# Selected rows taken batch by batch: the first batch's attention among the first attention's units, its feed-forward beside the last ranks, the second batch's attention with keys and values

## The chip, the cores and the metric

The kernel runs on one core of one Trainium2 chip. The metric is the device time of one execution in microseconds (us). Three runs of the kernel before took 1828.56, 1829.37 and 1838.12 us (median 1829.37). A fourth execution was profiled; all views below are of that one.

## What is computed

Two layers of a gated model on x of shape (2, 2048, 512), each with a cross-attention onto a context of 128 tokens and a feed-forward; every part is added to x through tanh of a gate. Cut to what matters here:

```python
x = x + tanh(g_xattn[0]) * L0_xattn(layernorm(x), ctx)   # 16 heads of 32
x = x + tanh(g_ffn[0]) * L0_ffn(layernorm(x))
x = x + tanh(g_xattn[1]) * L1_xattn(layernorm(x), ctx)   # 16 heads of 64
x = x + tanh(g_ffn[1]) * L1_ffn(layernorm(x))            # ternary weights, convolution

def L0_ffn(x):
    _, idx = top_k(x @ w_router, 256)             # of each batch's 2048 rows
    x_sel = x[idx]
    h = rmsnorm(x_sel, g1)
    x_attn = causal_attention(h) @ W_out.T        # 16 heads of 32, 256 rows
    h2 = rmsnorm(x_sel + x_attn, g2)
    x_ff = (silu(h2 @ W1.T) * (h2 @ W2.T)) @ W3.T # 1365 hidden columns
    return x with rows idx set to x_sel + x_attn + x_ff
```

So only 256 rows of each batch go through the attention and feed-forward of `L0_ffn`. The other rows get a cheap affine step. Which rows are selected is known for a batch only when all of its 2048 scores are.

## The kernel before, in words

All x rows are held as tiles of 128 rows by 512 columns, 32 of them; four make a block of 512 rows, and there are eight blocks, four for each batch. All matrix products are float32, but for the ternary feed-forward of the second layer and the counting of ranks (bfloat16). PE below is TensorE, with PEld its weight loads; DVE is VectorE, ACT ScalarE, POOL GpSimd, SP SyncE, whose queue issues nearly all DMAs, in order.

**First attention** (`cross_attention`, called at L647). It runs over 128 units, a unit being one head of one block (L338). A unit does scores (L271), softmax (a maximum on DVE L116, four exponentials on ACT L119, a reciprocal on DVE L127, a multiplication on POOL L128), transposes of the probabilities (L289) and, for four heads together, values (L297). The front of the next block, that is its norm and its transposed rows (L110), is issued at unit 8 of a block (`ahead`), the queries (L248) group by group, and the output products (L315) of a finished block are spread over the units after it. Products for queries, output and row transposes go through a pool of two PSUM buffers (`ps_mm`), transposes and values through another of two (`ps_o`), scores through one of four (`ps_sc`).

**Router and ranks.** When a block's output is done, `after_block` (L649) puts a generator `router` (L447) into `pending`. `beside` (L441) advances it by two steps in each unit. It takes the norm's statistics and the router's score of each row, writes the rows to `x1_d` and the rows after the affine step to `x_d`, and then counts each row's rank by comparisons on DVE (L511) and matmuls with ones (L517). After the last block of a batch, `gather` (L591) turns ranks into row indices (L597, L601, L617) and fetches the 256 rows into `xs` by an indirect DMA on POOL's queue (L619). The second batch's last router, ranks and gather run in a loop of their own after the units (L651).

**Selected rows** (L659 to L985), both batches side by side, 512 columns wide. Weights are loaded (L718, L722, `load_ffn` L665), masks built on POOL, then: norm of the rows, transposes (L110), values (L751), and for each of four chunks of four heads queries and keys (L769), scores with mask for either batch (L788, L798, L799), exponentials (L804), a multiplication on POOL (L814), transposes (L824), values (L829). Then output (L852), the second norm (L694, L698, L703), and the feed-forward in eleven steps of 128 hidden columns: up and gate (L952), SiLU and product (L960, L962), down (L938). Beside the feed-forward the second layer's two weight matrices are made ternary (`ternary`, L879): load, sum of absolute values on ACT, a sum across partitions on PE (L901), and integers on ACT and DVE. The results are added into `x_d` by indirect DMAs (L979).

**Keys and values of the second attention** (`W1.keys_values()` at L989; L182, L200), and then that attention with the ternary feed-forward's first half as a second stream of work (`beside4`), and at the end the second half.

**What sets the order.** The program is written in terms of tiles; a scheduler puts each engine's instructions into one fixed order and adds the waits. The order of the Python code gives the priority: what is issued earlier stands earlier where it can. A tile pool with so many buffers makes the next user of a buffer wait for the last reader of it, and a pool that is opened where another was closed waits for the instructions that used that place.

Of the kernel before, what the change touches and what calls it, by code (L numbers as in the profile page):

```python
# [10 lines left out]
F32 = mybir.dt.float32  # L11
BF16 = mybir.dt.bfloat16
# [31 lines left out]
def flamingo_kernel(ctx: ExitStack, tc: tile.TileContext, a: dict, out: bass.AP):  # L44
# [28 lines left out]
    dramp = ctx.enter_context(tc.tile_pool(name="dramp", bufs=1, space=bass.MemoryType.DRAM))  # L73

# [61 lines left out]
    class CrossWeights:  # L136
# [38 lines left out]
        def keys_values(self):  # L175
            L, nE, bias = self.L, self.nE, self.bias
            with ExitStack() as st:
                ps0 = psum_pool(st, L + "ps0", 2)
                for e in range(nE):
                    pk = ps0.tile([P, B * M], F32, name="pk", tag="pk")  # L180
                    for c in range(CC):
                        nc.tensor.matmul(  # L182
                            pk,
                            self.wk[:, c, ts(e, P)],
                            self.ctxT[:, c, :],
                            start=(c == 0),
                            stop=(c == CC - 1),
                        )
                    src = pk.rearrange("p (b m) -> p b m", b=B)
                    if bias:  # L190
                        nc.vector.tensor_scalar(
                            self.kT[:, :, e, :], src, self.bk[:, e : e + 1], None, ALU.add
                        )
                    else:
                        nc.vector.tensor_copy(self.kT[:, :, e, :], src)
                for b in range(B):
                    for n in range(nE * P // 512):
                        pv = ps0.tile([P, 512], F32, name="pv", tag="pv")
                        for c in range(CC):
                            nc.tensor.matmul(  # L200
                                pv,
                                self.ctxT[:, c, ts(b, M)],
                                self.wv[:, c, ts(n, 512)],
                                start=(c == 0),
                                stop=(c == CC - 1),
                            )
                        to = self.v[:, b, ts(n, 512)]
                        if bias:
                            nc.vector.tensor_tensor(to, pv, self.bv[:, ts(n, 512)], ALU.add)
                        else:  # L210
                            nc.scalar.copy(to, pv)
# [179 lines left out]

    with ExitStack() as st:
        xres = st.enter_context(tc.tile_pool(name="xres", bufs=1))
        x = [xres.tile([P, D], F32, name=f"x{i}") for i in range(NT)]
        rp = st.enter_context(tc.tile_pool(name="router", bufs=1))
# [39 lines left out]
        def load_x(i):  # L435
            for t in range(i * TB, (i + 1) * TB):
                nc.sync.dma_start(out=x[t], in_=x_in[t])

        pending = []

        def beside(u):  # L441

            for _ in range(2):
                while pending and next(pending[0], pending) is pending:
                    pending.pop(0)

        def router(n, tiles):  # L447
# [6 lines left out]
            for i in range(TB):  # L454
# [4 lines left out]
                ws = act.tile([P, D], F32, name="ws2", tag="ws2", bufs=1)  # L459
# [21 lines left out]
            for i in range(TB):  # L481
                yield
                xo = act.tile([P, D], F32, name="xo", tag="xo", bufs=2)
# [7 lines left out]
                nc.sync.dma_start(out=x_d[b][ts(t0 + i - b * TPB, P), :], in_=xo)  # L491
            yield
# [98 lines left out]
        def gather(b):  # L591
# [26 lines left out]
            for r in range(2):  # L618
# [7 lines left out]
                )  # L626

        W0 = CrossWeights("L0_", D // P, True, gx[0], st, "left")
        with ExitStack() as st0:
            W0.load_context(st0, "left")  # L630
            load_x(0)
            W0.load_rest()
            for i in range(1, B * NBLK):
                load_x(i)
            W0.keys_values()
        act = st.enter_context(tc.tile_pool(name="L0_act", bufs=2))
        row = st.enter_context(tc.tile_pool(name="L0_row", bufs=8))
        ps_mm = psum_pool(st, "L0_mm", 2)
        ps_sc = psum_pool(st, "L0_sc", 4)
        ps_o = psum_pool(st, "L0_o", 2)  # L640

        def stage1_rows(n):
            tiles = x[n * TB : (n + 1) * TB]
# [4 lines left out]
            W0, act, act, ps_mm, ps_sc, ps_o, row, 2, 8, stage1_rows,  # L648
            lambda n, tiles: pending.append(router(n, tiles)), beside,  # L649
        )  # L650
        while pending:  # L651
            beside(None)


    right, right1, right2 = ExitStack(), ExitStack(), ExitStack()
    step = const.tile([P, 2], F32, name="step")
    finstep = const.tile([P, 1], F32, name="finstep")
    w2_d = dramp.tile([P, HC, D], BF16, name="w2_d")
    with ExitStack() as st:  # L659
        AHEAD = 3  # L660
        wst = st.enter_context(tc.tile_pool(name="wst", bufs=AHEAD))
        keepp = st.enter_context(tc.tile_pool(name="keepp", bufs=1))
        w13 = {}

        def load_ffn(f):  # L665
            n = min(P, DFF - f * P)
            w1c = wst.tile([P, DC, P], F32, name="w1c", tag="w1c")
            nc.sync.dma_start(
                out=w1c[:, :, :n], in_=row_tiles(a["W1T"])[:, :, ds(f * P, n)]
            )  # L670
            w2c = wst.tile([P, DC, P], F32, name="w2c", tag="w2c")
            nc.sync.dma_start(
                out=w2c[:, :, :n], in_=row_tiles(a["W2T"])[:, :, ds(f * P, n)]
            )
            w3c = wst.tile([P, D], F32, name="w3c", tag="w3c")
            nc.sync.dma_start(out=w3c[:n, :], in_=a["W3T"][ds(f * P, n), :])
            w13[f] = (w1c, w2c, w3c)

        g1 = keepp.tile([P, DC], F32, name="g1")
        nc.sync.dma_start(out=g1, in_=a["g1"])  # L680
        g2 = keepp.tile([P, DC], F32, name="g2")
        nc.sync.dma_start(out=g2, in_=a["g2"])
        xa = [keepp.tile([P, D], F32, name=f"xa{i}") for i in range(4)]

        def wide(name):
            return keepp.tile([P, DC, BLK], F32, name=name, tag="wide", bufs=2)

        def rms_block(tiles, gcol, dst, pool, ps, tag, name, r=None):

            hn = [pool.tile([P, D], F32, name="hn", tag="hn", bufs=4) for _ in tiles]  # L690
            if r is None:
                ss = pool.tile([P, 4], F32, name=name + "_ss", tag="rms_ss")
                for i, t in enumerate(tiles):
                    nc.scalar.activation(hn[i], t, AF.Square, accum_out=ss[:, i : i + 1])  # L694
                rs = rsqrt(4, ss, 1.0 / D, 1e-6, small, name + "_r")
                r = [rs[:, i : i + 1] for i in range(4)]
            for i, t in enumerate(tiles):
                nc.vector.tensor_scalar(hn[i], t, r[i], None, ALU.mult)  # L698
            transpose_block(
                ps,  # L700
                tag,
                hn,
                lambda d, pt: nc.vector.tensor_scalar(  # L703
# [732 lines left out]
```

## Time and profile before

| | us |
|---|---|
| median of 3 runs | 1829.37 |
| the profiled execution | 1832.29 |
| its span, first to last instruction | 1830.2 |
| PE busy | 1663.7 |
| DVE busy | 1278.9 |
| ACT busy | 1046.0 |
| POOL busy | 524.2 |
| last output product of the first attention ends | 512.3 |
| first row transposes of the second attention | 813.4 |

The page of the profile gives busy times by engine, then the span in 40 slices (45.8 us each here) as digits of tenths. The busy time of PE is modelled and holds the latency of matmuls, so a busy PE need not be at its peak; the granted clock beside it says how fast its clock was let run (1.00 is full). A line of the instructions in order of time has the start, the length of the merged run, engine, line, operation, output tile<-inputs, shape, number of records, and in brackets the idle time of the engine before it and what ended it. Every float32 matmul shows as two records, each with its weight load.

### The profile page before, as it was taken

The page shows a single profiled execution, that of the slowest core. Times are in us where ns is not written, and L with a number is a line of the kernel's source. Part 1 is how long each engine was busy: PE and PEld are TensorE (multiplying, and loading weights), DVE is VectorE, ACT ScalarE, POOL GpSimd, SP SyncE. Part 2 cuts the span into 40 slices and gives each one's busy share as a digit, 9 for nine tenths or more (in the row PEclk, how much of TensorE's full clock was granted, in tenths as well). Part 3 has the DMA queues.
Part 4 walks back from the last instruction along what each step waited for, and adds up shares of the span by engine and source line. Part 5 has one row for each costly group of instructions (what it writes and reads, how often), then busy time and mean ns, then how long its engine had stood idle before and what let it go on. Part 6 is the DMA issues. An engine that isn't in the chain of part 4 may idle for free.

```text
span 1830.2 us, 24658 instructions
## 1 busy us (share of the span) xinstructions
PE 1663.7 (91%) x7836; PEld 832.5 (45%) x7882; DVE 1278.9 (70%) x2591; ACT 1046.0 (57%) x3057; POOL 524.2 (29%) x668
## 2 busy tenths in 40 slices
PE   6989998899958989989999999999998999898969
PEld 3544444444424444445544444544444454443423
DVE  5777777977674622234447789799888888876966
ACT  1654545355402526115447778778777887854566
POOL 4543344253211210042224243322424243221200
PEclk9989989999968889989999999999999999999989
DMA  8010001010152037240011234234143133155475
GB/s 291 7 41 35 30 35 41 24 47 36 53 191 102 1 123 236 81 115 24 7 41 64 87 115 147 93 135 141 48 155 113 81 101 130 69 206 214 144 237 189
DMA packets 98455, 184.36 MB, mean 101 GB/s; under 512 B 11327, under 2 KB 30527, under 8 KB 94614
## 3 DMA queue, kind: packets, MB, share of 16 engines
q1 hardware_dynamic: 97430, 180.70, 28.5%
q0 software_dynamic: 896, 2.10, 0.6%
q8 instruction: 62, 1.02, 0.2%
q14 instruction: 67, 0.55, 0.1%
HBM read 108.31 MB, written 74.45 MB: 100 GB/s over the span
## 4 chain that ended last, share of the span: by engine, by line
PE 36%; DVE 12%; DMA 6%; ACT 5%; issue 2%; POOL 2%; SPq 1%; POOLq 0%; DVEq 0%; ACTq 0%
PE pp L315 8%; PE pq L248 8%; PE ph L1079 3%; DVE h L1095 3%; PE po L297 2%; PE sc L271 2%; PE pu L952 2%; PE acc L938 2%; PE pw L952 2%; PE tp L289 2%; PE po L1308 2%; DMA x<-h_d 1%; DMA h_d<-h 1%; DMA hf<-h_d 1%; DMA hq<-hq_d 1%
## 5 line engine op out<-in xcount | busy, mean ns | idle before, releaser
L119 ACT ACTIVATE A<-sc,nmx 128x128 f32<-128x128 f32 x1024 | 363.6, 382 | 147.8 <-DVE nmx L116 122.5
L128 POOL TENSOR_TENSOR A<-A,rden 128x512 f32<-128x512 f32 x256 | 274.6, 1075 | 471.5 <-DVE rden L127 361.6
L315 PE MATMUL pp<-L_wo,OT 128*128 128x512 f32 x768 | 362.4, 604 | 4.9 <-DVE u L1089 4.5
L248 PE MATMUL pq<-xnT,L_wq 128*128 128x512 f32 x768 | 346.7, 600 | 0.2 <-ACT xnT L237 0.2
L119 ACT ACTIVATION_READ_ACCUMULATOR A<-sc,nmx 128x1 f32 x1024 | 225.9, 221 | 0.0
L116 DVE TENSOR_REDUCE nmx<-sc 128x4 f32<-128x512 f32 x256 | 168.2, 678 | 82.6 <-PE sc L271 82.5
L290 DVE COPY AT<-tp 128x512 f32<-128x512 f32 x256 | 172.8, 677 | 65.5 <-PE tp L289 64.9
L248 PEld LDWEIGHTS pq<-xnT,L_wq 128*128 128x128 f32 x768 | 143.8, 192 | 161.7 <-issue 154.0
L315 PEld LDWEIGHTS pp<-L_wo,OT 128*128 128x128 f32 x768 | 136.4, 192 | 148.3 <-issue 134.3
L289 PE MATMUL tp<-ident,A 128*128 128x128 f32 x1024 | 167.0, 288 | 35.7 <-POOL A L128 32.1
L1095 DVE SCALAR_TENSOR_TENSOR h<-u,cw,h 128x512 f32<-128x512 f32 x256 | 191.4, 782 | 6.0 <-ACT h L1091 5.6
L289 PEld LDWEIGHTS tp<-ident,A 128*128 128x128 f32 x1024 | 121.5, 145 | 105.9 <-issue 48.6
L271 PEld LDWEIGHTS sc<-L_kT,qT 32*128 32x128 f32 (+1 forms) x2048 | 117.8, 197 | 89.7 <-issue 69.1
L271 PE MATMUL sc<-L_kT,qT 32*128 32x128 f32 (+1 forms) x2048 | 147.7, 301 | 10.0 <-DVE qT L256 7.7
L1308 PE MATMUL po<-w2q,hq 128*128 128x512 bf16 x501 | 120.3, 392 | 19.9 <-DVE hq L1290 8.2
L1091 ACT ACTIVATE h<-u,cb,cw 128x512 f32<-128x512 f32 x128 | 99.2, 809 | 64.3 <-DVE u L1089 58.8
L297 PE MATMUL po<-AT,L_v 128*32 128x512 f32 (+1 forms) x512 | 121.2, 671 | 9.8 <-DVE AT L290 8.1
L305 ACT COPY OT<-po 128x512 f32<-128x512 f32 x96 | 55.8, 589 | 122.7 <-PE po L297 122.2
L1079 PE MATMUL ph<-xiT,w1q 128*128 128x512 bf16 x477 | 122.8, 381 | 2.7 <-DVE u L1089 0.5
L1089 DVE TENSOR_TENSOR u<-ph,inv_b 128x512 f32<-128x512 f32 x128 | 84.9, 683 | 31.8 <-PE ph L1079 27.5
L1088 POOL COPY u<-carry 128x2 f32<-128x2 f32 x128 | 49.7, 390 | 196.2 <-DVE h L1095 168.4
L311 POOL TENSOR_TENSOR x<-x,L_bo 128x512 f32<-128x512 f32 x64 | 86.2, 1364 | 32.1 <-DMA x<-x_d 17.1
(233 smaller groups left out, 2189.2 us busy)
## 6 DMA issues: line engine op xcount, KB each, us to landing
h_d<-h SPq DMA_DIRECT2D x28, 1024.0 KB, 4.2
x_d<-x SPq DMA_DIRECT2D x64, 256.0 KB, 7.4
hf<-h_d SPq DMA_DIRECT2D x64, 256.0 KB, 3.2
x<-x_d SPq DMA_DIRECT2D x61, 256.0 KB, 4.6
x<-h_d SPq DMA_DIRECT2D x48, 256.0 KB, 4.2
x<-in_x SPq DMA_DIRECT2D x32, 256.0 KB, 5.4
x_d<-xo SPq DMA_DIRECT2D x32, 256.0 KB, 2.0
xf<-x_d SPq DMA_DIRECT2D x32, 256.0 KB, 4.1
```

The source lines that it names most:

```text
L116: nc.vector.tensor_reduce(nmx, sc, AX.X, ALU.max, negate=True)
L119: nc.scalar.activation(out_tile[:, h, :], sc[:, h, :], AF.Exp, bias=nmx[:, h : h + 1], accum_out=den[:, h : h + 1],)
L128: nc.gpsimd.tensor_tensor(out_tile, out_tile, rden.unsqueeze(2).to_broadcast([P, n, width]), ALU.mult,)
L248: nc.tensor.matmul(pq, W.wq[:, d, ts(e, P)], xnT[:, d, :], start=(d == 0), stop=(d == DC - 1),)
L271: nc.tensor.matmul(sc[h][:, t, :], qT[e % cpg][r, ts(t, P)], W.kT[r, b, e, :], start=True, stop=True,)
L289: nc.tensor.transpose(tp[:, t, :], A[:, t, :], ident)
L290: nc.vector.tensor_copy(AT, tp.rearrange("p t n -> p (t n)"))
L297: nc.tensor.matmul(po[h * dh : (h + 1) * dh, :], W.v[:, b, ts(hd, dh)], AT[c * hpc + h], start=True, stop=True,)
L315: nc.tensor.matmul(pp, OT[e][:, ts(i, P)], W.wo[:, e, :], start=(e == 0), stop=(e == nE - 1),)
L1079: nc.tensor.matmul(ph, w1q[:, d, ts(c, P)], xiT[g][:, d, :], start=(d == 0), stop=(d == DC - 1),)
L1095: nc.vector.scalar_tensor_tensor(z, u[:, ds(k, BLK)], cw[:, c, k : k + 1], z, ALU.mult, ALU.add)
L1308: nc.tensor.matmul(po, rows(c), w2q[:, c, :], start=(c == 0), stop=(c == HC - 1))
```

## The change

Each batch's selected rows go through by themselves, 256 columns wide. `selected_attention(b, ...)` and `feed_forward(b, ...)` take the place of the code for both; the first is a generator whose steps are issued between those of something else. The operations are the same; up, gate, queries and keys are now twice as many matmuls of 256 columns, and their weights are loaded once for each batch.

1. The first batch's attention is put among the units of the first attention. After its gather, `gather(0)` waits four steps and then puts the generator into `selecting`; `beside` advances it by one step in each unit. It uses `ps_mm` for products and scores (two heads at a time) and `ps_o` for transposes and values, with one buffer for each of its own tiles (`bufs` = 1). To make room, the first attention keeps three blocks of x instead of eight: a block is loaded when the router has done with the one three before it. The transposed rows have one buffer instead of two, and the next block's front comes at unit 10 instead of 8.
2. After the units comes the first batch's feed-forward. Between its steps are issued what is left of the routers (four steps at a time), the second batch's ranks and gather among it, and `ternary(1)`, the second ternary matrix.
3. Then the second batch's attention, with its own PSUM pools, four heads at a time and two buffers for each tile; at every second step of it one group of the second attention's keys and values.
4. Then the second batch's feed-forward with `ternary(0)`, and the second attention.

The mask and the norms' gains are made at the start of the kernel (`selected_constants`), and the rows' scatter is made for each batch.

The core of the diff:

```diff
-        def keys_values(self):
+        def keys_values(self, mm):
...
+                yield
...
+    def selected_attention(b, mm, sc_tile, o_tile, together, pools, bufs):
...
+        qk, behind = (yield from queries_keys(0)), None
+        for c in range(DC):
+            A = yield from probabilities(*qk)
+            if bufs == 1:
+                yield from values(A, c)
+            if c + 1 < DC:
+                qk = yield from queries_keys(c + 1)
+            if bufs > 1:
+                if behind:
+                    yield from values(*behind)
+                behind = A, c
...
+        h2T[b] = wide("h2T")
+        yield from rms_rows(rows, g2, h2T[b], mm, pool)
...
+    def feed_forward(b, ps_acc, mm, work):
...
+        for f in range(AHEAD):
+            load(f)
+        for f in range(NF):
...
+            if f > 0:
+                down(f - 1)
+                if f - 1 + AHEAD < NF:
+                    load(f - 1 + AHEAD)
+            for w, n in work:
+                for _ in range(n):
+                    next(w, None)
+        down(NF - 1)
+        for w, _ in work:
+            for _ in w:
+                pass
...
+    xres = router_stack.enter_context(tc.tile_pool(name="xres", bufs=3 * TB, side="right"))
...
         def beside(u):
             for _ in range(2):
                 while pending and next(pending[0], pending) is pending:
                     pending.pop(0)
+            for q in selecting:
+                next(q, None)
...
+            load_x(n + 3)
             yield
             yield from ranks(b, blk)
...
+            if b == 0:
+                for _ in range(4):
+                    yield
+                mm = in_pool(ps_mm, "mm")
+                selecting.append(
+                    selected_attention(0, mm, mm, in_pool(ps_o, "o"), 2, sel_pools, 1)
+                )
...
         cross_attention(
-            W0, act, act, ps_mm, ps_sc, ps_o, row, 2, 8, stage1_rows,
+            W0, act, act, ps_mm, ps_sc, ps_o, row, 1, 10, stage1_rows,
             lambda n, tiles: pending.append(router(n, tiles)), beside,
         )
-        while pending:
-            beside(None)
+        for q in selecting:
+            for _ in q:
+                beside(None)
...
+        feed_forward(
+            0,
+            psum_pool(sp, "s2a_acc", 1),
+            mm,
+            [(router_rest(), 4), (ternary(1, mm, *raw), 1)],
+        )
...
+        second = selected_attention(
+            1, mm, in_pool(ps_sc, "sc"), in_pool(ps_o, "o"), 4, selected_pools(sp), 2
+        )
+        keys_values = W1.keys_values(mm)
+        for k, _ in enumerate(second):
+            if k == 2:
+                W1.load_rest()
+            if k % 2:
+                next(keys_values, None)
...
+        feed_forward(1, psum_pool(sp, "s2c_acc", 1), mm, [(ternary(0, mm, *raw), 1)])
...
-    W1.keys_values()
```

## The prediction

> **What bounds the kernel now.** I read the page first (busy shares, then the TensorE rows), then a table of busy time cut at the borders of the stage that changes, then the instructions in order of time at each hole in it.
>
> ```profile
> PE 1663.7 (91%) x7836; PEld 832.5 (45%) x7882; DVE 1278.9 (70%) x2591; ACT 1046.0 (57%) x3057; POOL 524.2 (29%) x668
> ...
> PEclk9989989999968889989999999999999999999989
> ```
>
> TensorE (PE) is the busiest engine by far, and nearly all of the chain that ended last is its matmuls. The one deep hole in its granted clock lies in slices 12 to 15, around the selected rows. Cut there (start:end, length, then busy us of PE, PEld, DVE, ACT and POOL, granted clock, DMA share, GB/s):
>
> ```profile
> 372.00:512.30 140.30, 129.11 (x718) 64.21 (x716) 104.55 (x236) 67.32 (x305) 48.09 (x45) 0.94 0.13 48
> 512.30:541.90 29.60, 14.87 (x78) 7.38 (x77) 25.11 (x74) 3.51 (x5) 2.93 (x4) 0.61 0.58 196
> 541.90:558.00 16.10, 4.08 (x16) 3.07 (x17) 6.35 (x16) 0.00 (x0) 4.07 (x9) 0.50 1.02 365
> 558.00:663.70 105.70, 96.31 (x547) 47.53 (x546) 50.66 (x110) 46.88 (x164) 25.37 (x25) 0.92 0.03 12
> 663.70:783.80 120.10, 119.47 (x284) 53.87 (x285) 32.10 (x64) 42.73 (x60) 0.87 (x1) 0.96 0.52 168
> 783.80:804.70 20.90, 20.82 (x73) 13.49 (x71) 5.57 (x13) 1.79 (x4) 11.53 (x14) 1.00 0.70 151
> 804.70:813.40 8.70, 0.03 (x1) 0.06 (x1) 4.11 (x11) 0.55 (x1) 5.44 (x5) 0.73 0.36 121
> 920.00:1550.00 630.00, 606.38 (x2684) 301.64 (x2712) 512.45 (x960) 484.99 (x1190) 205.51 (x309) 0.99 0.31 104
> ```
>
> The rows are, in order: the last third of the first attention; the last block's router and ranks, which are VectorE work (25.1 of 29.6 us) with PE half idle; the gather of the second batch and its layer norm; the selected attention of both batches; the feed-forward; keys and values; the front of the second attention; and, for comparison, that attention in its steady state. Everything from 512.3 to 813.4 (301.1 us) runs one thing after the other. Where PE stands in it (last bracket: idle before, and what ended it):
>
> ```profile
> 554.57 1.30 PE L110 MATMUL ptr<-ident,hn 128*128 128x128 f32 x4 [11.60 <-DVE hn L698]
> ...
> 663.66 1.94 PE L110 MATMUL ptr<-ident,hn 128*128 128x128 f32 x8 [4.06 <-DVE hn L698]
> ...
> 783.80 10.53 PE L182 MATMUL pk<-L_ctxT,L_wk 128*128 128x256 f32 x48
> 794.16 10.46 PE L200 MATMUL pv<-L_wv,L_ctxT 128*128 128x512 f32 x24
> 813.37 2.01 PE L110 MATMUL ptr<-ident,xf 128*128 128x128 f32 x8 [8.75 <-issue]
> ```
>
> The 11.60 us are the rows of the second batch arriving, the 8.75 us the reload of x after the last scatter. A float32 matmul is two records. From the second two lines: 512 columns take 0.43 us a record, 256 columns 10.36/48 = 0.216 us (10.36 is this group's entry in the chain of waits).
>
> **PE work at full rate.** A 512-column float32 matmul is 0.86 us. Both batches' selected attention: 64 of them (16 values, 32 queries and keys, 16 output) 55 us; its scores 7.5 (0.94 per 16 records), probabilities' transposes about 11.5, values 8.6, row transposes 4.3: 87 us, that is 43.5 per batch. Feed-forward: eleven steps of 3.43 us each for up, gate and down: 113, that is 57 per batch. Keys and values 20.7. The last block's rank matmuls about 12. In 301.1 us there are 233 us of work; 68 are holes and slow clock.
>
> **The change, part by part.**
>
> *The split itself.* The program's PE order shows as much work as before: up, gate, queries and keys become twice as many matmuls of half the width. The Trainium skill ("TensorE: Matmul & The Clock Gate", section "Back-to-back issue gap") speaks against this: in a stream of weight loads and matmuls the spacing is set by both, so short matmuls wait for their weights. The nearest row is the keys' matmul above, 256 columns with a fresh weight load each: its load takes 190 ns and its spacing is 216, so the load is just hidden. By the rule's direction, with loads exposed, the 88 extra matmuls of the feed-forward would cost 88 x 2 x 0.19 = 33 us; by the row 0. I take the row, with 3 us for the upper end. Weights are fetched twice (about 8.4 MB more for the feed-forward, 4 MB for the attention); the first attention's DMA share is 0.13, so there it is covered.
>
> *First batch's attention beside the first attention (step 1).* Its 43.5 us leave the serial stretch and enter the last 140 us. By the same prices that stretch holds about 115 us of PE work (79 wide matmuls 68, transposes 17, scores 9, values 10, ranks and row transposes 11), so it runs at 115/140 = 82%. How well it fills is not in the trace. Lower bound: it packs as the steady second attention, which has a filler stream: its blocks hold about 101 us of work in 105 us, 96%: (115+43.5)/0.96 = 165, +25 us. Upper bound: it stays at 82%: 193, +53 us. The selected attention alone ran at 87/105.7 = 82%, and here it goes with single buffers through the same two PSUM buffers for products (ps_mm) and two for transposes (ps_o), so I go nearer to the upper end: 86.5%, 183 us, +43. VectorE does not bind on average: 104.6 + about 33 (half of 50.7 + 6.4, with narrower tiles) in 183 us is 75%. Over the last 30 us it will be close, since ranks, router and the tail of the selected attention all fall there. Its waits stand in PE's queue: behind each are the units' scores and transposes, and behind those ScalarE's exponentials. SP takes its weight loads between the stores of x; PE reuses each weight tile only about seven units later, so those are hidden. The mask building on POOL (1.1 us) moves to the start, where PE waits for its first weights until 11.3 us: nothing. The single xnT and the transposes two units later: the second attention runs so already at 96%, so nothing; if the queries wait, up to the 2.4 us once seen per block for such a copy.
>
> *First batch's feed-forward beside the last ranks (step 2).* PE's order is: feed-forward steps 0 and 1, the score broadcast, step 2, the rank matmuls, the gather's index matmuls, and steps 3 and 4 among the latter. The first weights load only once the attention's last transposes free their place: some 3 us of wait (a 256 KB load lands in 4.8 us, 3.4 us of output matmuls cover part). So the broadcast comes at about 3 + 6.9 + 1.7 = 12 us instead of 5.8, and the chain from it to the row index (518.06 to 541.09, 23 us, VectorE) ends at 35 us. By then PE has done 4.5 of 11 steps, 23 us. The other 34 follow: it ends at about 70 us. The gather (7.5 us to the rows) and the norm lie under them. Bounds: 62 (ranks almost free) to 80: weights, the raw w2, its stored integers and the keys' weights are 18 MB, 61 us at the 300 GB/s that the stretch from 680 to 700 us shows, and the stores of w2 stand in SP's queue before the weights of the last steps.
>
> *Second batch's attention with keys and values (step 3).* 43.5 + 20.7 = 64; 3 for the clock (0.92 in that stage before); start without a hole, since key matmuls stand in front and the rows are there. The tail is exposed: from the last scores through 5 us of VectorE, the exponentials, three POOL multiplications of 1.04, transposes, values, output, square, the 1.0 us power and back is about 22 us with 13 of PE work: 9 us of hole; another 4 for weight tiles queued behind 4 MB of the second attention's weights. 82 us; bounds 72 to 88.
>
> *Second feed-forward and the next front (step 4).* 57, plus 4 us: the ternary sum waits for 4.8 MB, 16 us at 300 GB/s plus latency and the last ScalarE sum, while PE reaches it after 15.5. The rows of the second attention's first block depend on the first batch's scatter alone, and their norm stands on VectorE before the last products: the 8.7 us go. 61 us; bounds 58 to 64. ScalarE changes its table twice more (1.28 us each), beside PE work.
>
> **Sum.** 301.1 becomes 70 + 82 + 61 = 213, that is 88 us less; step 1 costs 43 of them back; 45 remain. Span 1830.2 - 45 = 1785; the profiled execution took 1832.3 with a span 2.1 shorter, and stands 2.9 above the median 1829.4: about 1784 to 1785 against the median. What is late next is the same engine: PE, in the first attention.
>
> **Rivals.** *A, it packs like the second attention:* step 1 at +25 gives a gain of 63, 1766. For it: PE waits little in that stretch. Against it: single buffers.
>
> *B, loads and the rank chain hold the split feed-forward:* step 2, 3 and 4 near their upper ends (+19), step 1 at +53: gain 16, 1813. For it: 1.02 DMA share at 541.9 when loads pile up. Against it: the loads are three steps ahead.
>
> *C, slower: the hand-offs of the selected attention block PE's queue.* It makes about 40 of them in the first attention (32 of queries, keys, scores, transposes, values; 8 of rows and outputs), each a PE instruction that waits in order for VectorE, ScalarE or POOL with the units behind it. To eat the 45 us each must stop PE for 1.1 us. From 60 to 512 us the present ones of that kind do so:
>
> ```profile
> PE tp L289 <- POOL A L128: 21.8, 12, 2.9
> ```
>
> (total, times, longest): 1.8 us each. If all 40 did, 72 us: 1856. Against it: most of the 112 such transposes in that time did not wait at all.
>
> *D, it does not do what it says:* PE's order has steps 0 to 2 ahead of the ranks and keys among the second attention, so the mixing is there; what may fail is only its size, which is B.
>
> **Chances.** Forecast 0.58; A 0.18; B 0.17; C 0.07. The range leaves out C and the tails of A: 1760 to 1815. About 0.5% (9 us) is what a measurement of this kernel can tell from no change. Faster 0.87 (forecast, A, most of B); same 0.07; slower 0.06.
>
> **What would show it.** Step 1: last output matmul of the first attention 43 us later (about 555); wrong if under 530 or over 575. Step 2: no gap over 5 us at the gather, feed-forward end 70 us later. Step 3: a PE gap of about 9 us before the second feed-forward's transposes. Step 4: under 2 us between the last down product and the second attention's first transposes. From there on the time to the end is as before, 1017 us; if that moves by over 10 us, something that I left out is at work.

## The result, and the profile after

| | before | after |
|---|---|---|
| median (7 runs each) | 1831.83 us | 1814.7 us |
| span of the profiled execution | 1830.2 us | 1813.0 us |
| first attention's last output product ends | 512.3 | 559.9 |
| first row transposes of the second attention | 813.4 | 782.9 |
| from there to the end | 1016.8 | 1030.1 |

The ratio is 0.9902, with a 95% interval of 0.9879 to 0.9925: 18 us faster, where 45 were forecast. The page of the profile:

```profile
PE 1662.9 (92%) x8076; PEld 879.3 (49%) x8122; DVE 1296.7 (72%) x2639; ACT 1052.9 (58%) x3074; POOL 525.7 (29%) x669
...
PEclk9999999999999999989999999999999999998989
```

The deep hole in the granted clock (slices 12 to 15) is gone. Slice 18 has an 8 in both kernels, but not for the same reason: before, it held the gap ahead of the second attention; now it begins at 771 us (17 x 45.3) and holds that attention's start, which has no gap ahead of it. Cut at the new borders (start:end, length, then busy us of PE, PEld, DVE, ACT, POOL, granted clock, DMA share, GB/s):

```profile
372.00:559.90 187.90, 175.07 (x1002) 95.47 (x999) 134.49 (x314) 86.17 (x366) 56.04 (x53) 0.94 0.15 49
559.90:641.00 81.10, 71.86 (x299) 48.86 (x297) 39.75 (x104) 26.39 (x41) 5.76 (x6) 0.92 0.85 287
641.00:718.30 77.30, 68.83 (x392) 44.08 (x392) 32.69 (x86) 27.75 (x89) 15.83 (x15) 0.97 0.33 103
718.30:782.90 64.60, 61.39 (x223) 44.30 (x223) 20.94 (x48) 22.87 (x36) 1.01 (x1) 0.93 0.58 175
782.90:842.70 59.80, 52.33 (x218) 29.71 (x216) 21.00 (x45) 23.59 (x95) 25.43 (x26) 0.83 0.23 62
```

The rows are the first attention's end with the first batch's attention in it; the first feed-forward; the second batch's attention with keys and values; the second feed-forward; and the second attention's first block, from its row transposes to those of block 1. The holes in TensorE's order at the places that the prediction named:

```profile
641.06 1.13 PE L184 MATMUL pk<-L_ctxT,L_wk 128*128 128x256 f32 x4 [1.05 <-DVE xa L670]
...
716.47 1.91 PE L437 MATMUL ptr<-ident,hn 128*128 128x128 f32 x8 [3.68 <-DVE hn L431]
...
782.90 1.26 PE L113 MATMUL ptr<-ident,xf 128*128 128x128 f32 x10
```

The second attention's transposes stand right behind the last down product, without the 8.75 us gap of before. But the block that they open is the slow one: before, its transposes and those of block 1 were 47.4 us apart (813.4 to 860.7), now 59.8. The row of before for the same block:

```profile
813.40:860.70 47.30, 47.30 (x216) 26.67 (x216) 19.23 (x44) 23.77 (x95) 11.41 (x11) 0.94 0.07 23
```

TensorE was busy for all of it; now it has 52.3 busy us in 59.8, at a lower clock. The later blocks differ by at most 2.5 us either way and the end by 4.7, in all by 0.8.

Beside the forecast's terms, these stretches are: step 1 47.6 for 43 (4.6 more), step 2 81.1 for 70 (11.1 more), step 3 77.3 for 82 (4.7 less), step 4 64.6 for 61 (3.6 more), and the rest, which was to stay, 13.3 more. Together 27.9, which is the 45 of the forecast less the 17.2 by which the profiled spans differ, to 0.1. These are single executions. In a second profile of the changed kernel (run 12 below) the five differences are 11.1, 10.5, -6.4, 2.0 and 10.9: step 2 and the rest are large in both, while step 1 can't be read to a few us.

**POOL at the start of the second attention.** First the changed kernel, then the kernel before (start, length, instruction, and in brackets POOL's idle time and what ended it):

```profile
783.74 1.63 POOL L672 DMA_INDIRECT x_d<-xa,idx  x1 [22.04 <-DVE xa L671]
790.38 1.56 POOL L672 DMA_INDIRECT x_d<-xa,idx  x1 [5.00 <-DMA xf<-x_d]
795.59 0.19 POOL L1177 MEMSET carry<- 128x32 f32 x2 [3.65 <-DMA x_d<-xa,idx]
...
798.25 2.99 POOL L315 TENSOR_TENSOR x<-x,L_bo 128x512 f32<-128x512 f32 x2 [1.03 <-DMA x<-x_d]
801.49 7.37 POOL L315 TENSOR_TENSOR x<-x,L_bo 128x512 f32<-128x512 f32 x6 [0.26 <-DMA x<-x_d]
808.81 2.05 POOL L131 TENSOR_TENSOR A<-A,rden 128x512 f32<-128x512 f32 x2
```

```profile
796.16 0.19 POOL L1104 MEMSET carry<- 128x32 f32 x2 [3.64 <-DMA x_d<-xa,idx]
...
799.08 2.49 POOL L311 TENSOR_TENSOR x<-x,L_bo 128x512 f32<-128x512 f32 x2 [2.30 <-DMA x<-x_d]
801.73 7.37 POOL L311 TENSOR_TENSOR x<-x,L_bo 128x512 f32<-128x512 f32 x6 [0.16 <-DMA x<-x_d]
```

It is the same sequence both times: the last batch's scatters, a memset of memory that they had occupied, which waits for the second to land, then eight additions of the output bias to residual rows (blocks 0 and 1). The second scatter starts 6.6 us after the first. Both add to the same tensor, so I take it that it waits for the first to land; the bracket names a load that landed at that moment. The rows for the additions are late too: their loads were issued only from 795.5 us, when the second scatter had landed. Before, all of it lay under keys and values and under the front gap, and was over at 809, 4 us before the block began. Now it begins with the block, and the first multiplication of probabilities (A<-A,rden) waits behind it in POOL's order until 25.9 us into the block. What TensorE makes of that (last bracket: its idle time):

```profile
802.31 2.07 PE L275 MATMUL sc<-L_kT,qT 64*128 64x128 f32 x14 [1.94 <-ACT A L122]
809.92 2.11 PE L293 MATMUL tp<-ident,A 128*128 128x128 f32 x8 [5.54 <-POOL A L131]
```

### The profile page after: what moved, and what is told of

It reads as the page before. It is cut to its first block, busy times and chain, and to the rows that moved or that the text cites. A ratio compares the mean times of both kernels' runs of the same rounds, so it can differ in the third digit from the quotient of the medians.

```text
span 1813.0 us, 25255 instructions
## 1 busy us (share of the span) xinstructions
PE 1662.9 (92%) x8076; PEld 879.3 (49%) x8122; DVE 1296.7 (72%) x2639; ACT 1052.9 (58%) x3074; POOL 525.7 (29%) x669
## 4 chain that ended last, share of the span: by engine, by line
PE 52%; DVE 23%; ACT 8%; DMA 7%; issue 4%; POOL 4%; SPq 0%; POOLq 0%; DVEq 0%; ACTq 0%
PE pp L319 13%; PE pq L252 10%; PE sc L275 4%; PE po L301 4%; PE tp L293 4%; PE ph L1152 3%; ACT A L122 3%; DVE h L1168 3%; DVE nmx L119 2%; DVE AT L294 2%; DVE marks L859 2%; PE pu L645 2%; PE pw L645 2%; PE acc L630 2%; PE po L1381 2%
## 5 line engine op out<-in xcount | busy, mean ns | idle before, releaser
L319 PE MATMUL pp<-L_wo,OT 128*128 128x512 f32 x768 | 366.3, 608 | 10.7 <-DVE x L328 5.6
```

Source lines behind the costliest of these rows:

```text
L319: nc.tensor.matmul(pp, OT[e][:, ts(i, P)], W.wo[:, e, :], start=(e == 0), stop=(e == nE - 1),)
```

## The experiments

Theory P: the missing 12.4 us of the first block are POOL's queue at its start. Theory V: the first feed-forward is too long because VectorE, in its fixed order, holds TensorE. Rivals: R, the first block is late for its own reasons (loads, normalization, clock); L, loads hold the feed-forwards; C, mixing among the units doesn't pay. Ratios are to the kernel before, run beside each on the same chip; the changed kernel's were 0.9902 and, in a second set of runs, 0.9909.

**1. Late scatters.**

```
-            nc.vector.tensor_scalar(t, t, gf[0], None, ALU.mult)
+            to = hold_tile() if b else t
+            nc.vector.tensor_scalar(to, t, gf[0], None, ALU.mult)
...
+    def late_scatter(i, OT, act):
+        at = act.tile([P, 1], mybir.dt.uint32, name="late_idx", tag="late_idx")
+        nc.vector.scalar_tensor_tensor(
+            at, OT[:, 0:1], 0.0, late_row[:, i : i + 1], ALU.mult, ALU.add
+        )
+        scatter(1, i, at)
```

To keep the outputs until then, the edit also opens the second attention's `hold` pool ahead of the second feed-forward (not shown).

> Edit: the scaled outputs of the second batch's selected rows go to a buffer that outlives the feed-forward, and their two scatters wait for results of the second attention's units (one in unit 11, one in unit 15), so that they no longer stand at the head of POOL's queue and nothing of the second attention waits for their memory. Theory P (the scatters, and what stands behind them in POOL's queue, make the second attention's first block 12.4 us longer than before, 59.8 us between the transposes of blocks 0 and 1 against 47.4): this stretch falls by 8 to 12 us, the kernel from 1814.7 to about 1804. Rival R (the first block is late for its own reasons: its rows' loads, DVE's normalization, ACT, a slow clock): the stretch and the time stay within 2 us.

Measured: 1804.28 us, 0.9834 (0.981 to 0.9858). The first block takes 48.1 us (59.8). POOL in it:

```profile
786.75 1.27 POOL L315 TENSOR_TENSOR x<-x,L_bo 128x512 f32<-128x512 f32 x1 [2.21 <-DMA x<-x_d]
790.86 1.28 POOL L315 TENSOR_TENSOR x<-x,L_bo 128x512 f32<-128x512 f32 x1 [2.83 <-DMA x<-x_d]
792.24 1.04 POOL L90 TENSOR_TENSOR L_ln_rstd<-L_ln_rstd_e,neghalf 128x4 f32<-128x4 f32 x1
793.23 8.13 POOL L315 TENSOR_TENSOR x<-x,L_bo 128x512 f32<-128x512 f32 x6
801.45 1.04 POOL L131 TENSOR_TENSOR A<-A,rden 128x512 f32<-128x512 f32 x1
```

The additions start 4.7 us into the block (it starts at 782.05) and not 15.4, and the first multiplication comes at 19.4 us, no longer at 25.9. Theory P holds, R falls. One profile each would be little to go by, but all others agree: the first block takes 58.0 to 59.8 us in the seven profiles in which scatters and additions stand as in the changed kernel, and 47.9 to 48.6 in the four with late scatters. Late scatters also let the rows for the additions be loaded from 783.8 us on; how much is POOL's order and how much these loads was not told apart.

**2. No bias additions in the first two blocks.**

```
-                nc.gpsimd.tensor_tensor(t, t, W.bo, ALU.add)
+                if bias or n > 1:
+                    nc.gpsimd.tensor_tensor(t, t, W.bo, ALU.add)
```

> Edit: the second attention leaves out adding its output bias to the residual rows of its blocks 0 and 1 (part of the computation left out); these eight POOL additions took 10.4 us between the normalization's power and the first multiplication of probabilities. The scatters stay. Theory P: the first multiplication, which was ready at 802.5 us and ran at 808.8, runs when ready, and the first block gets 5 to 7 us shorter; what remains of the 12.4 us, 5 to 7 us, is the scatters' and the memset's share. If the scatters were all of it: 0 to 1 us. Rival R: 0 to 1 us.

Measured: 1803.52 us, 0.9832 (0.9809 to 0.9855); first block 46.9 us. The scatters stand where they stood and are waited for:

```profile
788.65 1.56 POOL L673 DMA_INDIRECT x_d<-xa,idx  x1 [4.91 <-DMA xf<-x_d]
793.45 0.19 POOL L1178 MEMSET carry<- 128x32 f32 x2 [3.25 <-DMA x_d<-xa,idx]
...
799.46 1.04 POOL L131 TENSOR_TENSOR A<-A,rden 128x512 f32<-128x512 f32 x1 [4.38 <-DVE rden L130]
```

I had expected 5 to 7 us from the additions and as much from the scatters. The shares don't add: either edit alone gives all of it. With either, POOL is free by the time the probabilities are there, 18 to 19 us into the block; only both together run past that. And what is lost then is more than the waits, as the block's windows show, first of the changed kernel, then with late scatters (granted clock is the third number from the end):

```profile
782.90:800.00 17.10, 17.10 (x66) 8.66 (x65) 7.91 (x17) 4.53 (x7) 6.56 (x10) 1.00 0.60 143
800.00:812.00 12.00, 4.53 (x25) 3.43 (x25) 3.65 (x8) 6.77 (x34) 10.60 (x9) 0.59 0.28 103
812.00:824.00 12.00, 12.00 (x31) 7.18 (x31) 3.19 (x8) 3.43 (x17) 4.11 (x4) 0.55 0.01 1
824.00:842.70 18.70, 18.70 (x100) 10.45 (x99) 6.24 (x13) 8.86 (x38) 4.16 (x4) 1.00 0.00 1
```

```profile
800.00:812.00 12.00, 9.86 (x53) 6.24 (x54) 5.49 (x14) 9.94 (x51) 7.61 (x8) 1.00 0.01 2
812.00:830.00 18.00, 18.00 (x98) 10.22 (x96) 6.24 (x13) 8.69 (x37) 4.16 (x4) 1.00 0.00 1
```

TensorE waits 7.5 us (1.94 + 5.54) against 2.6 (1.70 + 0.18 + 0.74) with late scatters: 4.9 us. The other 7 are the clock, which in the changed kernel is at half rate from the first wait until about 823 us. A run of 14 score records takes 2.07 us at half rate; in run 1, after 1.70 us of waiting, it takes 1.16 at a clock of 1.00.

**3. Keys and values back behind the second feed-forward.**

```
-            if k % 2:
-                next(keys_values, None)
-        for _ in keys_values:
-            pass
...
     sel_stack.close()
+    with ExitStack() as sp:
+        for _ in W1.keys_values(in_pool(psum_pool(sp, "L1_ps0", 2), "kv")):
+            pass
```

> Edit: the keys and values of the second attention go back behind the second feed-forward, alone, as before; all else as in the changed kernel. Theory P: they cover the scatters again, so the second attention's first block falls from 59.8 to about 47.4 us (-12.4); the second batch's attention loses their 20.7 us of matmuls but bares 4 to 10 us of hand-offs, which the keys and values covered; they stand at the end with 20.7 us and some gap. Together -8 to +2 us against the changed kernel. If moving the keys and values paid what I had forecast (that they fill holes and cost nothing later), the kernel is 4 to 10 us slower. Rival R: the first block stays at about 59.8 us.

Measured: 1814.47 us, 0.9887 (0.9866 to 0.9909): the changed kernel's within the error, and its span is 1813.3 for 1813.0. The first block is back at 46.2 us, and the front gap is back too (total wait, times, longest):

```profile
PE ptr L113 <- DVE xf L104: 8.8, 1, 8.8
```

This balances the account of that step. The second batch's attention alone takes 60.9 us (640.5 to 701.4), with keys and values inside it 77.3: the mixing saves 4 us of 20.7. The front gap saves 8.8. The first block gives back 13.6 (59.8 - 46.2). So all that moving keys and values gained (4 and 8.8) was returned a few microseconds later.

**4. Statistics held behind a gated product.** In the first feed-forward VectorE waits, in its fixed order, for the gathered rows of the second batch, with a gated product (gT) queued behind. First VectorE, then TensorE (which needs gT for its down product), in the changed kernel:

```profile
609.31 0.69 DVE L99 BATCH_NORM_STATS2 lns_st<-xs 128x6 f32<-128x512 f32 x1 [5.30 <-DMA xs<-x_d,idx]
...
613.46 0.42 DVE L655 TENSOR_TENSOR gT<-pw,su 128x256 f32<-128x256 f32 x1
```

```profile
613.93 3.22 PE L630 MATMUL acc<-w3c,gT 128*128 128x512 f32 x4 [3.31 <-DVE gT L655]
616.95 2.39 PE L645 MATMUL pu<-h2T,w1c 128*128 128x256 f32 x8
619.17 1.89 PE L645 MATMUL pw<-h2T,w2c 128*128 128x256 f32 x8
```

```
+        if behind is not None:
+            for i in range(n):
+                nc.vector.tensor_copy(st[:, i, 0:1], behind[:, 0:1])
...
+            if b == 0 and f == 6:
+                marker[1] = keepp.tile([P, 1], F32, name="marker")
+                nc.vector.tensor_copy(marker[1], gT[f][:, 0:1])
```

> Edit: the statistics of the second batch's gathered rows (VectorE) are made to depend on the gated product of the seventh feed-forward slice, so that VectorE no longer waits for the gather ahead of the sixth slice's gated product. Theory V (VectorE's order holds the first feed-forward: 3.3 us of waiting at 613.9 us, then some 1.5 us at half clock): the first feed-forward falls from 80 to about 75 us, the kernel by 4 to 5 us. Rival L (the weights' loads hold it, with the DMA engines at 0.83 to 0.87): the gap comes back as a wait for the next weights, and the feed-forward stays within 1.5 us of 80.

Measured: 1815.2 us, 0.9891 (0.9868 to 0.9915). The feed-forward's last product ends 74.9 us after its first one begins, for 80.1: theory V, and no wait for weights came in its place. But the time as a whole hardly moved, which I had not expected. In this profile the first attention ended 8 us later; runs 9 to 12 ask why.

**5. Ranks spread wider** (with the statistics held behind the ninth slice's product).

```
-            [(router_rest(), 4), (ternary(1, mm, *raw), 1)],
+            [(router_rest(), 2), (ternary(1, mm, *raw), 1)],
```

> Edit: in the first feed-forward two steps of the last ranks per slice in place of four, so that the ranks lie beside slices 3 to 9 and not 2 to 4; the second batch's statistics stay behind a gated product, here the ninth slice's. Theory V (the first feed-forward's 80 us hold 9 us in which TensorE waits for VectorE: 4.4 us of it between 580 and 590 us, where the counting matmuls stand in TensorE's order right behind the marks that VectorE makes): against the run with the statistics alone held back (first feed-forward 75 us) another 2 to 4 us go, to 71 to 73 us, unless the gather, which now ends later, makes the second batch's first transposes wait. Rival L (the weights' loads pace it): 75 us or more, with waits for weights in place of the waits for marks.

Measured: 1814.0 us, 0.9887 (0.9863 to 0.9911); the feed-forward 75.1 us. A miss for V's second part: the waits of the counting matmuls for marks stayed (3.1 us in four, 3.0 in three without this edit). L misses as well, no weight is waited for. The last 5 us over the forecast's 70 were not taken out by any run. The traces show where TensorE loses time there: in the changed kernel five waits around the rank matmuls, 4.5 us in all (0.95, 1.02, 1.08, 0.78, 0.67), with the clock at half for 10.3 us (583.8 to 594.1); run 11 has the same five waits and 10.3 us at half.

**6. Step 1 undone.**

```
                 while pending and next(pending[0], pending) is pending:
                     pending.pop(0)
-            for q in selecting:
-                next(q, None)
```

> Edit: step 1 undone alone: the first batch's attention runs behind the first attention's units, with the routers' rest beside it, and no longer among them. Theory M (mixing pays: 43.5 us of TensorE work cost 47.6 us among the units, and alone it would leave the hand-offs between TensorE, VectorE, ACT and POOL bare): the first attention ends 47 us earlier, the attention alone with the ranks takes 65 to 75 us, the first feed-forward loses the ranks and falls to 68 to 72 us: together 7 to 18 us slower than the changed kernel. Rival C (the hand-offs block TensorE's queue among the units): not slower.

Measured: 1845.2 us, 1.0056 (1.0038 to 1.0074): 28 us slower than the changed kernel, and slower than the kernel before. The right side, but more than I had expected. The attention alone with the ranks, then the first feed-forward:

```profile
504.40:602.20 97.80, 71.77 (x397) 45.26 (x396) 58.60 (x162) 28.29 (x89) 18.65 (x20) 0.79 0.37 133
602.20:669.00 66.80, 62.21 (x222) 44.62 (x222) 15.99 (x37) 22.90 (x36) 0.00 (x0) 0.92 0.88 276
```

97.8 us for 65 to 75: TensorE is idle for 26 of them and its clock is 0.79. Among the units most of that is covered, so rival C falls. But the attention that runs alone here keeps the single buffers and the pairs of heads that were chosen for its place among the units, so the 28 us are the gain of that place over a version built for it, not over the best attention that could run alone.

**7. Late scatters and held-back statistics together.** The edits of 1 and 4.

> Edit: the late scatters and the held-back statistics together. Theories P and V (two separate costs at two places): the first feed-forward takes about 75 us and the second attention's first block about 48 us; the gains add, 10.5 + 5, to about 1799 us on the scale of 1814.7 for the changed kernel. If a stretch that loses its waits is given them back as a lower granted clock, as the unchanged total of the run with the statistics alone suggests, the time stays at about 1804 us.

Measured: 1803.64 us, 0.9833 (0.9813 to 0.9854), as late scatters alone. By stretches both gains are there (feed-forward 74.7, first block 48.6 us), but the first attention ended at 566.3 and not near 560.

**8. With the sum of absolute weights later.** In the changed kernel the second feed-forward has this wait, and two products slowed behind it:

```profile
738.30 0.59 PE L708 MATMUL wtot<-wsum,ones 128*128 128x8 f32 x2 [3.21 <-ACT wq L703]
738.74 3.76 PE L645 MATMUL pu<-h2T,w1c 128*128 128x256 f32 x8
742.30 2.86 PE L645 MATMUL pw<-h2T,w2c 128*128 128x256 f32 x8
```

```
+        if k == 0:
+            for _ in range(2):
+                yield
+            nc.vector.scalar_tensor_tensor(
+                sums[:, 0:1], marker[0], 0.0, sums[:, 0:1], ALU.mult, ALU.add
+            )
         tot = mm([P, 8], "wtot")
```

> Edit: as the one with late scatters and held-back statistics, and in the second feed-forward the matmul that sums the absolute weights is made to depend on the fifth slice's gated product, so that it no longer stands in TensorE's order before its loads have landed (3.2 us of waiting at 738.3 us in the changed kernel). Theory: the second feed-forward falls from 64.6 to 60 to 62 us, the kernel by 3 to 4 us against the one with two edits. Rival (the loads of that weight hold the feed-forward's own weights back too): the wait moves to a slice's weights, 0 to 1 us.

Measured: 1793.92 us, 0.9785 (0.9766 to 0.9803). The second feed-forward takes 58.3 us with TensorE busy for all of it: 6.3 us less, for a wait of 3.21; the rest is again the clock after the wait. The total fell by more than expected, 9.7 us, of which a part may be the spread between runs (their intervals are 3 to 4 us wide on each side).

**9 to 12. A control, and the best version.** In runs 4, 5, 7 and 8 the first attention ended at 566 to 568 us, and at 558 to 562 in the others that have step 1, with the same order on TensorE. All four had one small tile more, which by my reckoning moves many buffers by 32 bytes (no view shows addresses). So four kernels ran side by side: the changed kernel with an unused tile, the statistics without a tile of their own, the three edits without one, and the changed kernel again. The second pair of lines is the difference from run 4:

```
+    unused = keepp.tile([P, 1], F32, name="unused")
+    nc.gpsimd.memset(unused, 0.0)
...
-                marker[1] = keepp.tile([P, 1], F32, name="marker")
+                marker[1] = graw[:, 2:3]
```

> Edit: the changed kernel with one more tile of 4 bytes per partition, set once and never read; the orders of TensorE and VectorE are those of the changed kernel, but many buffers allocated behind it lie 32 bytes further (the transposed block, queries, probabilities, the feed-forward's weights). It is a control: in all four runs that hold the statistics back through such a tile, the first attention ended 4 to 8 us later than in the four without it, with the same waits and a lower granted clock in it. Theory S (the shifted addresses do that): the first feed-forward's first product stands at 565 to 569 us against 560 to 562, and the kernel is 3 to 6 us slower than the changed kernel. Theory G (the clock grants differ from run to run and the four agree by chance): 558 to 562 us, time as the changed kernel's within 2 us.

> Edit: the statistics of the second batch held back as before, but the value that they depend on is kept in an old, no longer used tile, so that no address moves. Theory S: the first feed-forward starts at about 560 us and takes 75 us, and the kernel gains the 4 to 5 us that the earlier run had lost again in the first attention: about 0.9975 of the changed kernel. If the shorter feed-forward costs clock elsewhere: start at 566 us and no gain. Theory G: the start lies anywhere from 558 to 568 us.

> Edit: late scatters, held-back statistics and the later sum of absolute weights together, with the two values that they depend on kept in an old tile, so that no address moves. Theory S: first feed-forward from 560 to 635 us, second attention's first block 48 us, and 4 to 5 us less than the run with the same three edits and its own tile: about 1789 us. Theory G or a clock that takes the gain back: 1792 to 1795 us.

> The changed kernel itself, unaltered, beside the others on the same chip, as the mark to read them against: 0.990 of the kernel before, its first feed-forward from 560 to 640 us. If the clock grants alone scatter the first attention's end (theory G), it may lie up to 8 us from that; under theory S it lies within 2 us.

| kernel | us | ratio (95%) | first feed-forward, start and length |
|---|---|---|---|
| unused tile | 1813.53 | 0.9879 (0.9851 to 0.9908) | 560.0, 80.2 |
| statistics, no tile | 1812.6 | 0.9884 (0.9857 to 0.991) | 564.0, 74.7 |
| three edits, no tile | 1791.45 | 0.9761 (0.9734 to 0.9788) | 566.3, 74.9 |
| changed kernel again | 1817.16 | 0.9909 (0.9885 to 0.9933) | 566.4, 79.4 |

Theory S (addresses) falls: the unused tile starts at 560.0, and the very same kernel, which started at 559.9, starts at 566.4. In the stretch from 350 to 430 us its two profiles read, first then second:

```profile
350.00:430.00 80.00, 74.20 (x424) 41.51 (x423) 62.69 (x156) 39.73 (x171) 32.12 (x30) 0.98 0.20 67
```

```profile
350.00:430.00 80.00, 74.38 (x405) 41.08 (x404) 61.10 (x153) 36.09 (x157) 28.67 (x27) 0.91 0.20 63
```

The same busy time, fewer records done, a lower granted clock. TensorE's waits from 100 to 560 us, added up by what they waited for, are the same in both within half a microsecond each. So the end of the first attention scatters by some 10 us between executions, and single profiles can't settle differences there. The feed-forward's length can be read from them: 77.9 to 80.4 us in the six profiles with the statistics in their old place, 74.7 to 75.1 in the six with them held back. Whether those 5 us reach the total, the times don't tell: 0.9884 to 0.9891 with the statistics alone, 0.9879 to 0.9909 for the changed kernel with and without the unused tile.

The three edits together are the best version: 0.9761, 43.6 us under the kernel before, run beside it (1835.05). Its windows, from the first feed-forward on:

```profile
566.30:641.20 74.90, 69.93 (x299) 48.22 (x297) 38.73 (x107) 26.45 (x41) 4.73 (x5) 0.93 0.90 304
641.20:717.60 76.40, 66.99 (x393) 42.77 (x393) 33.84 (x87) 27.77 (x89) 16.10 (x15) 0.99 0.35 111
717.60:775.90 58.30, 58.30 (x223) 42.34 (x223) 20.62 (x50) 22.33 (x36) 1.01 (x1) 0.98 0.64 194
775.90:824.00 48.10, 45.59 (x218) 25.36 (x216) 24.16 (x45) 23.51 (x95) 22.67 (x24) 1.00 0.19 66
```

## Why the prediction was wrong

The direction was right, the size was not: 18 us for 45. Two terms make up most of what is missing: what follows the first transposes of the second attention (13.3 us of 27.9) and step 2 (11.1). The step that failed with the larger share is in step 4: "The rows of the second attention's first block depend on the first batch's scatter alone, and their norm stands on VectorE before the last products: the 8.7 us go." They went, and 12.4 us came back inside the first block, of which run 1 takes out 11.7 and run 2 all. The time from there to the end I had put at no change, without a reason. I followed the block's rows to its first transposes and stopped there. I asked neither what else lay under the 8.75 us and under keys and values, nor what stands ahead of the probabilities in POOL's order. The profile of before held the answer: its bias additions end at 809 us, inside the gap that I was striking out. My own check named the symptom: if the time from there to the end "moves by over 10 us, something that I left out is at work". It moved by 13.3.

Point by point:

- *Step 1, +43.* One profile shows 47.6. The twelve profiles, of this and the edited kernels, in which it is among the units start the first feed-forward at 558 to 568 us, so the price is 46 to 56 against the one profile of before: above my value, and about at my upper bound of 53. Undoing it costs 28 us (run 6); with these buffers, this part pays.
- *Step 2, 70.* Measured 80 (81.1 to the keys' first product), at my upper bound of 80. The 3 us of wait for the first weights did not come. The chain of the ranks to the row index ended later than I had put it: the index was cast at 602.07, 42 us after the start, for 35. Its last 2.7 us are VectorE's order once more: the row was known at 599.3, but ahead of the cast stood a conversion of ternary weights that waited 2.14 us for a store. I wrote that the gather and the norm "lie under" the remaining slices. For TensorE's rows that is so; for VectorE's order it isn't: 5 of the 10 us are the statistics waiting for the gather ahead of a gated product (runs 4, 7, 9 to 12). It is the same kind of omission as on POOL.
- *Step 3, 82.* 77.3. The hole at the tail was 3.68 us and not 9. My own terms (64, 3, 9 and 4) add up to 80, not 82.
- *Step 4, 61.* 64.6. I put the wait for the ternary sum at 4 us. It was 3.21, but it cost 6.3 (run 8): I counted a wait at its length and left out the slow clock behind it.
- *The split itself.* Taken as free, and it is: in the best version eleven slices of 256-column products take 58.3 us with TensorE busy throughout, for 57 of work at full rate. The exposed loads that I read from "Back-to-back issue gap" in "TensorE: Matmul & The Clock Gate" would have added some 16 us to each feed-forward (half of 33).

Of the rivals, B named the right size (1813) by luck, and half of the cause: the rank chain did hold the first feed-forward, through VectorE, but the weights' loads did not, and no term of B is what came back in the second attention. B's step 3 is 11 us too long (88), which stands in for most of the 13.3 that it lacks. That 1814.7 lies inside my range (1760 to 1815) is luck as well: the range reaches so far only to take in B. In the changed kernel loads held TensorE once, through the ternary sum, which I had counted. C is refuted by run 6. A would have needed step 1 at +25.

That the three edits reach 43.6 us doesn't make the forecast right: it describes a kernel with three waits taken out, two of which the forecast had not seen and the third of which it had priced too low.

## What to carry to other kernels

Before striking out a gap, list for every engine what ran under it; the work that it covered is due at once when it goes, and an in-order queue puts it ahead of whatever comes next. Ask this also of the statistics, additions and memsets that a scheduler has moved forward: an early place in an engine's order is a wait for everyone behind it if its data is late. Price a wait on TensorE above its length: taking one out gave 5.2 us for 3.31 here, 6.3 for 3.21 and 11.7 for 4.9. Compare stretches only against the scatter between executions of one kernel.

## What the hardware showed unexpectedly

- A wait of TensorE goes on costing after it ends, and in steps. Read in windows of 0.1 us, the granted clock of the changed kernel is at 0.50 for 3.4 us at the wait of 3.31 us in the first feed-forward (614.5 to 618.0), for 6.8 at the one of 3.21 in the second (737.4 to 744.2), for 10.3 at the short waits of the ranks and for 20.5 in the first block (802.3 to 822.8). Other profiles show 17.1 there, and 3.4 for 1.8 us of waiting (run 12, second feed-forward). All are multiples of 3.4 us, and the length of a wait alone doesn't say which: 1.7 us slowed the clock for 3.4 us in run 7's first block and not at all in run 1's.
- In the first block, the last 13 us at half rate come behind the second wait, with TensorE busy all that time. "TensorE: Matmul & The Clock Gate" of the Trainium skill (section "What's actually happening") says that the rate is restored after about 3.4 us of sustained work. The first feed-forward agrees with that, the block doesn't: by the rule it would have lost some 7 us (4.9 of waits and 1.7 of clock), and it lost 12. What counts as busy in those 13 us, which hold scores on half the rows, transposes and two query products, was not tried. In all seven profiles with this stall the full rate came back within the 14 records of query products that follow (from 818.9 us here).
- One kernel's first attention, with the same order and waits, ended at 559.9 us in one execution and at 566.4 in another, by the granted clock alone.
